# New node states turned by VectorE in 32x32 blocks, with x and the result moved in runs of 32 channels, and aggregation in four tiles

## The chip, the cores and the metric

The kernel runs on one core of one Trainium2 chip. The metric is device time in microseconds (us), the median of several runs: 2050.7 us for the kernel before (three runs, 2047.82 to 2055.25).

## The reference

Inputs are x (128 graphs, 128 nodes, 256 channels), adj (128 x 128 x 128, zeros and ones) and the weights of two layers, all in float32. Cut to what matters:

```python
# layer 0
h = relu(layernorm(x))
x_conv = relu(bn2(conv17(relu(bn1(conv1(h))))) + h)        # along the nodes
x_nmp  = exp(-dist(h @ w_se)) * adj @ relu(h @ w_msg + b_msg)
r, z   = sigmoid(...), sigmoid(...)                         # of [x_conv, x_nmp] @ w_ih + h @ w_hh
n      = tanh(gi_n + r * gh_n)
x      = x + (1 - z) * n + z * h                            # the new state
# layer 1, only on nodes 0 to 24
h = relu(layernorm(x))
for g, idx in enumerate(GROUPS):                            # 5 groups of nodes, 53 rows together
    A   = sym_normalized(adj[idx, idx] + I)
    hid = relu(A @ (h[idx] @ W1[g]) + b1[g])
    out = relu(A @ (hid @ W2[g]) + b2[g])
    x[idx] += softmax(fusion_w)[g] * out
```

Nodes 25 to 127 leave layer 1 as they came into it. So the kernel stores nodes 32 to 127 (96 of 128) right after layer 0, and only the first 32 nodes go on.

## The kernel before, in words

**Stages.** Stage A (layer norm, first convolution, Fourier transform along the nodes) and stage B (the 17-tap convolution as products per frequency) run twice, for two halves of the graphs. Beside them `early` makes the messages and aggregates of layer 0. Then stage C (`stage_c`, line 687) makes the gates and the new state, for 32 groups q of four graphs (GB = 4), 512 columns each, with channels on the partitions. Layer 1 (`prepare`, `block`, line 1009) runs in 8 blocks of 16 graphs beside stage C.

**What sets the order.** All engines run in program order, and the program order is written by a planner, `Order.run` (line 183). Each piece of work is a generator in a lane; it yields a pair: what the step costs TensorE in us, and how long to wait until its next step may be placed. The planner takes the lane that has had least (cost over weight) among those whose next step is due. In the last phase (line 1137) the lanes are `loads`, `groups` (stage C, two groups at a time), `beside`, `rows`, and `second` (layer 1, weight 0.2). A step that yields a small wait, as those of the wn products do (lines 833 to 853, 0.2 us), lets one step of another lane in. A DMA stands in its queue at the place where the planner put its step. SP's queue issues in order: a DMA that has to wait keeps back all behind it.

**End of a group in stage C.** r holds the sums for tanh. Line 855 (ScalarE) does tanh, lines 858 to 861 (POOL) make d = (h - n) * z and z = d + n, first for channels 128 to 255 (dc = 1), then for dc = 0. The last add reads columns in order (graph j, 32-node run t, node n) and writes (t, j, n). The tile d has the tag of u2 and u3, so the next group's u2 (line 766, ScalarE, a copy of the accumulator p1) takes the buffer of d with dc = 0. TensorE then goes on accumulating into p1 at line 788. Eight transposes on TensorE (line 878) turn z into rows of (graph, node), four tiles t by two halves dc, VectorE adds x to them from tile xt (lines 881 to 884), for t = 0 into the layer 1 state X1, and POOL's queue stores t = 1 to 3 (line 887). xt has one buffer and was loaded one group of steps earlier (line 809, `load_x`, four DMAs on SP, runs of 256 channels); its load waits until the stores of the group before have left the tile. A step after 11 us, before which the planner may place other work, separates the new state from the transposes (line 865).

**W1 in layer 1.** `block` takes the node groups in turn: `first(g)` is the hidden product (line 1038), `second(g)` the one with W2 (line 1047). `load_w1` (line 926, SP) loads W1 of group g + 2 into the buffer that `first(g)` has left, and its place in the program is right before `first(g + 1)` (line 1059). Two buffers hold W1.

**Aggregation in layer 1** is `gather` (line 1075): graphs lie in pairs a = 0, 1, and s = 0, 1 is the graph in its pair, at partitions 64 s. Both input and output of a product lie at partitions 64 s, so the four products use two 64 x 64 corners of the array, twice each. One PSUM tile takes all four. `fuse` (line 1086) folds the 53 rows to 32 nodes for each a.

Of the kernel before, what the change touches and what calls it, by code (L numbers as in the profile page):

```python
# [9 lines left out]
FP = mybir.dt.float32  # L10
AF = mybir.ActivationFunctionType
ALU = mybir.AluOpType
# [3 lines left out]
B, N, D = 128, 128, 256  # L16
# [3 lines left out]
P = 128  # L20
GB = 4
# [9 lines left out]
SB = 16  # L31
QS = SB // GB
# [6 lines left out]
NR = sum(SIZES)  # L39
NN = 25  # L40
RP = 64
WIDE = 32
# [50 lines left out]
def _constants():  # L93

    row_node = [n for g in GROUPS for n in g]
    row_group = [i for i, g in enumerate(GROUPS) for _ in g]
    fwd, inv, tap = _fourier()
    parts = {
        "ident": np.eye(P),
        "mhalf": np.full((P, 8), -0.5),  # L100
        "fwd": fwd, "tap": tap, "inv": inv,
        "ones2": np.kron(np.eye(2), np.ones((RP, RP))),
        "et": np.zeros((P, 2 * RP)),
        "same": np.zeros((P, RP)),
        "diag": np.zeros((P, RP)),
        "e4": np.zeros((P, P)),
        "s2": np.zeros((P, 2 * WIDE)),
        "grp": np.zeros((P, NG)),
        "sgrp": np.zeros((P, 2 * NG)),
        "grpt": np.zeros((P, P)),  # L110
        "sel": np.zeros((P, P)),
        "emb": np.zeros((P, 12)),
    }

    roles = {0: [(2, 2, 0), (0, 0, 1), (1, 1, 0), (0, 0, 1)],
             1: [(0, 0, -1), (0, 0, 1), (1, 1, 0), (1, 1, 0)],
             2: [(1, 1, 0), (1, 1, 0), (0, 0, -1), (0, 0, 1)]}
    for j in range(GB):
        for role, factors in roles.items():
            for ch in range(3):  # L120
                k = WIDE * j + 3 * role + ch
                parts["sel"][ch, k] = 1
                parts["emb"][k] = np.array(factors).T.reshape(-1)
    for r, (n, g) in enumerate(zip(row_node, row_group)):
        for s in range(2):
            k = s * RP + r
            parts["et"][n, k] = 1
            parts["same"][k, [i for i in range(NR) if row_group[i] == g]] = 1
            parts["diag"][k, r] = 1
            for j in (s, s + 2):  # L130
                parts["e4"][k, j * WIDE + n] = 1
            parts["s2"][k, s * WIDE + n] = 1
            parts["grp"][k, g] = 1
            parts["sgrp"][k, s * NG + g] = 1
            parts["grpt"][g, k] = 1
    at, o = {}, 0
    for name, a in parts.items():
        at[name] = (o, o + a.shape[1])
        o += a.shape[1]
    return np.concatenate(list(parts.values()), 1).astype(np.float32), at  # L140
# [67 lines left out]
def kernel(ctx: ExitStack, tc: tile.TileContext, x, adj, consts, vecs, w_se, conv1_w,  # L208
                    conv2_w, w_msg, b_msg, w_ih, w_hh, W1, W2, b2, fusion_w, out):
    nc = tc.nc  # L210
# [7 lines left out]
    ptmp = ctx.enter_context(tc.tile_pool(name="ptmp", bufs=5, space=PSUM))  # L218
# [14 lines left out]
    def c(name):  # L233
        a, b = CAT[name]
        return cst[:, a:b]

    def v(name, i=None):
        a, b = VAT[name]
        return vec[:, a:b] if i is None else vec[:, a + i:a + i + 1]

    ident = c("ident")
# [15 lines left out]
    s2w = cp.tile([P, 2 * WIDE], FP, name="s2w")  # L257
# [106 lines left out]
    lab, turn = ExitStack(), []  # L364
# [14 lines left out]
    def load_x(t, q):  # L379
        for j in range(GB):  # L380
            nc.sync.dma_start(out=t[j * WIDE:(j + 1) * WIDE],
                              in_=x[q * GB + j].rearrange("(t n) c -> n t c", n=WIDE))
# [186 lines left out]
    EN, IN, IN2, X1, E_DONE, F_DONE = {}, {}, {}, {}, set(), set()  # L569
# [117 lines left out]
    def stage_c(q):  # L687
# [9 lines left out]
        fr = LATE["co"]  # L697
        xi = fr.tile([P, 2, 512], FP, tag="tc", name=f"xi{q}")
        xc = fr.tile([P, 2, 512], FP, tag="xc", name=f"xc{q}")
        for h in range(2):  # L700
            yt = IN2.pop((q, h))
            pi = ptmp.tile([P, 2, 2, 4, WIDE], FP, tag="tmp", name=f"pi{q}_{h}")
            for n in range(4):
                o = n % 2 * WIDE
                for w in range(4):
# [4 lines left out]
                        start=True, stop=True)  # L710
# [3 lines left out]
            s = slice(h * D, (h + 1) * D)  # L714
# [41 lines left out]
        r = fr.tile([P, 2, 512], FP, tag="r", name=f"r{q}")  # L756
# [44 lines left out]
        z = fr.tile([P, 2, 512], FP, tag="z", name=f"z{q}")  # L801
# [3 lines left out]
        sigmoid(z2, z2, 2)  # L805
        some_sums(q + 1, 2)
        yield 2.6, 0.0
        xt = fr.tile([P, 4, D], FP, tag="xt", name=f"xt{q}")
        load_x(xt, q)
        nc.vector.tensor_tensor(z1, u3, product(wrz, 3, xs), ALU.add)  # L810
        sigmoid(z1, z1, 2)
        nc.vector.tensor_tensor(vt, vb, product(wh, 3, xh, ptmp), ALU.add)
# [41 lines left out]
        for dc in (1, 0):  # L854
            nc.scalar.activation(r[:, dc], r[:, dc], AF.Tanh, bias=v("b_ih", 4 + dc))  # L855

            d = fr.tile([P, 512], FP, tag=f"u{2 + dc}", name=f"d{q}_{dc}")
            nc.gpsimd.tensor_sub(d, hT[:, dc], r[:, dc])  # L858
            nc.gpsimd.tensor_mul(d, d, z[:, dc])
            pat = "p (j t n) -> p t j n"  # L860
            nc.gpsimd.tensor_add(z[:, dc].rearrange("p (t j n) -> p t j n", t=4, j=GB),
                                 d.rearrange(pat, j=GB, t=4),
                                 r[:, dc].rearrange(pat, j=GB, t=4))
        G_DONE.add(q)
        yield 0.87, 11.0


        blk = q // QS
        while blk > 2 and blk - 3 not in F_DONE:
            yield 0.0, 0.5  # L870
        if blk not in X1:
            X1[blk] = fr.tile([P, QS, D], FP, tag="x1", name=f"x1_{blk}", bufs=3)
        for h in range(2):
            po = ptmp.tile([P, 2, D], FP, tag="tmp", name=f"po{q}_{h}")
            for i in range(2):
                t = 2 * h + i
                for dc in (1, 0):
                    nc.tensor.transpose(po[:, i, dc * P:(dc + 1) * P],  # L878
                                        z[:, dc, t * P:(t + 1) * P], ident)
            if h == 0:  # L880
                nc.vector.tensor_add(X1[blk][:, q % QS], xt[:, 0], po[:, 0])
                nc.vector.tensor_add(xt[:, 1], xt[:, 1], po[:, 1])
            else:
                nc.vector.tensor_add(xt[:, 2:], xt[:, 2:], po)  # L884
        yield 0.9, 1.5
        for j in range(GB):
            nc.gpsimd.dma_start(out=out[q * GB + j, WIDE:].rearrange("(t n) c -> n t c", n=WIDE),  # L887
                                in_=xt[j * WIDE:(j + 1) * WIDE, 1:4])
        C_DONE.add(q)


# [55 lines left out]
    def prepare(blk):  # L947

        while not (blk - 1 in P_DONE and blk - 2 in {-2, *B1_DONE}):
            yield 0.0, 1.0  # L950
        pool, pool2, b1 = S["pool"], S["pool2"], S["b1"]
        ac, r4 = S["ac"][blk % 2], S["r4"][blk % 2]
        aj = pool.tile([NN, SB, NN], FP, tag="dd", name=f"aj{blk}")
        nc.sync.dma_start(out=aj, in_=adj[blk * SB:(blk + 1) * SB, :NN, :NN]
                          .rearrange("b n m -> n b m"))
        yield 0.0, 4.0

        for r, n, w in _runs():
# [10 lines left out]
        for p in range(SB // 2):  # L969
# [30 lines left out]
        pr4 = ptmp.tile([P, QS, 2, RP], FP, tag="tmp", name=f"pr4{blk}")  # L1000
        nc.tensor.matmul(pr4.rearrange("p q a r -> p (q a) r"), c("e4"), ac,
                         start=True, stop=True)
        for j in range(GB):
            s = slice(j * WIDE, (j + 1) * WIDE)
            nc.vector.tensor_copy(r4[s, :, j, :], pr4[s, :, j // 2, :NR])
        yield 0.9, 1.0
        P_DONE.add(blk)

    def block(blk):
        while not (blk in P_DONE and blk - 1 in B1_DONE):  # L1010
            yield 0.0, 0.5
        pool, yz, b2row = S["pool"], S["yz"], S["b2row"]
        w2, ac, r4 = S["w2"], S["ac"][blk % 2], S["r4"][blk % 2]
# [46 lines left out]
        x1 = X1[blk]  # L1060
# [13 lines left out]

        def gather(q):
            zt = zts[q]
            pg2 = ptmp.tile([P, 2, D], FP, tag="tmp", name=f"pg2{blk}_{q}")
            for a in range(2):
                for s in range(2):
                    rows = slice(s * RP, (s + 1) * RP)  # L1080
                    nc.tensor.matmul(pg2[rows, a], ac[rows, 2 * q + a], zt[rows, a],  # L1081
                                     start=True, stop=True)
            nc.vector.tensor_tensor(zt, pg2, b2row[:, None, :].to_broadcast([P, 2, D]), ALU.add)
            nc.scalar.activation(zt, zt, AF.Relu)

        def fuse(q):
            zt = zts.pop(q)
            pf = ptmp.tile([P, D], FP, tag="tmp", name=f"pfu{blk}_{q}")
            for a in range(2):
                nc.tensor.matmul(pf[a * 2 * WIDE:(a + 1) * 2 * WIDE], s2w, zt[:, a],  # L1090
                                 start=True, stop=True)
            nc.vector.tensor_add(x1[:, q], x1[:, q], pf)
            b0 = blk * SB + q * GB
            if blk < NBLK - 1:
                nc.gpsimd.dma_start(out=out[b0:b0 + GB, :WIDE], in_=x1[:, q])
                return
            for j in range(GB):
                eng = nc.scalar if q == QS - 1 and j % 2 else nc.sync
                eng.dma_start(out=out[b0 + j, :WIDE], in_=x1[j * WIDE:(j + 1) * WIDE, q])

        for what, q in ((turn, 0), (turn, 1), (turn, 2), (gather, 0), (turn, 3), (gather, 1),
                        (gather, 2), (fuse, 0), (gather, 3), (fuse, 1), (fuse, 2), (fuse, 3)):
            what(q)
            if (what, q) == (gather, QS - 1):
                B1_DONE.add(blk)
            yield {turn: 0.45, gather: 0.9, fuse: 0.5}[what], 0.5
        F_DONE.add(blk)


# [70 lines left out]
```

## Time and profile before

| what | value |
|---|---|
| median of 3 runs | 2050.7 us |
| profiled execution, its own time | 2049.36 us |
| its span | 2047.5 us |
| granted TensorE clock, mean | 0.995 |
| stage C and layer 1 beside it | 676 to 1960 us of the span |
| the last two blocks of layer 1 alone | from 1960 us |
| DMA packets | 190148, of them 23626 under 512 B |
| queue of SP (q1) / of POOL (q0) | 156942 / 32656 packets |

The page gives for each engine the busy time and its share of the span. A group line tells the source line, engine, operation, shapes, count, total and mean time of one, and the idle time before it with the engine that ended it. The chain follows the last instruction back to what released it. A timeline row is start, duration, engine, line, operation, and in brackets how long the engine was idle before and who released it; rows of the same kind are merged, with xN. A matmul in float32 shows as two instructions, a transpose as one.

### The profile page before, as it was taken

How to read it: one execution, taken by the hardware profiler on the slowest of the kernel's cores; microseconds unless marked ns; L12 is line 12 of the kernel's file. 1: busy time of each engine (PE TensorE's matmuls, PEld its weight loads, DVE VectorE, ACT ScalarE, POOL GpSimd, SP SyncE). 2: the span in 40 equal slices, each digit the busy share in tenths (PEclk: the TensorE clock that was granted, in tenths of full speed). 3: DMA queues.
4: the chain of work that ended last, by engine and by line, in shares of the span. 5: the costliest groups of instructions: out<-in, count | busy, mean ns of one | idle time of the engine just before them, and what ended most of it. 6: DMA issues, size and time to landing. Idle time of an engine off the chain costs nothing.

```text
span 2047.5 us, 34132 instructions
## 1 busy us (share of the span) xinstructions
PE 2006.3 (98%) x12852; PEld 1659.2 (81%) x12852; DVE 1285.1 (63%) x2775; ACT 688.5 (34%) x1547; POOL 741.3 (36%) x898
## 2 busy tenths in 40 slices
PE   7998999999999999999999999999999999999998
PEld 5667888888888888878788788878888888878875
DVE  6774445875433676757756776777567667766742
ACT  4663222454222344222222332232232323222333
POOL 3552665333655032422422233233224323233230
PEclk9999999999999999999999999999999999999999
DMA  9997788645777544431323232332332233323121
GB/s 217 295 284 229 265 267 281 191 162 185 253 256 245 152 127 131 116 108 53 87 73 91 75 84 83 101 80 76 83 88 78 76 98 90 86 78 104 39 71 52
DMA packets 190148, 281.91 MB, mean 138 GB/s; under 512 B 23626, under 2 KB 143375, under 8 KB 189983
## 3 DMA queue, kind: packets, MB, share of 16 engines
q1 hardware_dynamic: 156942, 185.46, 31.7%
q0 software_dynamic: 32656, 93.98, 14.5%
q8 instruction: 102, 1.67, 0.3%
q14 instruction: 64, 0.52, 0.1%
q10 hardware_dynamic: 384, 0.28, 0.1%
HBM read 187.34 MB, written 92.27 MB: 137 GB/s over the span
## 4 chain that ended last, share of the span: by engine, by line
PE 89%; DVE 3%; issue 3%; POOL 3%; DMA 2%; ACT 1%; SPq 0%; POOLq 0%; DVEq 0%; ACTq 0%
PE p L735 39%; PE pa L526 7%; PE pm L630 5%; PE ph L1038 5%; PE pz L1047 5%; PE pc L421 4%; PE pb L526 3%; PE pf L432 3%; PE px L656 3%; PE pi L706 3%; PE pg L1081 1%; PE pw L474 1%; PE po L878 1%; PE ph L410 1%; PE py L1021 1%
## 5 line engine op out<-in xcount | busy, mean ns | idle before, releaser
L858 POOL TENSOR_TENSOR d<-hTc,r 128x512 f32<-128x512 f32 x64 | 87.2, 1362 | 299.3 <-ACT r L855 288.7
L526 PE MATMUL pa<-wf,X 128*128 128x256 f32 x640 | 152.2, 381 | 0.0
L716 DVE SCALAR_TENSOR_TENSOR xc<-xi,s_bn,hTc 128x256 f32<-128x256 f32 x128 | 148.1, 1195 | 2.3
L558 DVE SCALAR_TENSOR_TENSOR y<-pa,kk 128x512 f32<-128x512 f32 x78 | 53.8, 690 | 151.4 <-ACT kk L557 151.4
L887 POOL DMA_DIRECT2D out<-xt x128 | 72.2, 569 | 172.5 <-DVE xt L884 169.3
L750 ACT ACTIVATE z<-z,brz 128x256 f32<-128x256 f32 x128 | 58.1, 501 | 221.3 <-DVE z L804 187.9
L735 PE MATMUL p<-tm,wrz 128*128 128x256 f32 x512 | 132.3, 381 | 0.0
L735 PE MATMUL p<-th,wrz 128*128 128x256 f32 x512 | 132.1, 380 | 0.0
L735 PE MATMUL p<-tc,wrz 128*128 128x256 f32 x512 | 131.8, 380 | 0.0
L526 PEld LDWEIGHTS pa<-wf,X 128*128 128x128 f32 x640 | 118.1, 190 | 16.2 <-issue 2.0
L630 PE MATMUL pm<-wmsg,hT 128*128 128x256 f32 x512 | 123.3, 386 | 0.0
L421 PE MATMUL pc<-c1w,hTa 128*128 128x256 f32 x512 | 121.4, 383 | 1.2 <-ACT hTa L412 1.2
L1040 ACT ACTIVATE hh<-ph,vec 128x96 f32<-128x96 f32 (+3 forms) x160 | 64.4, 403 | 147.0 <-PE ph L1038 137.8
L1038 PE MATMUL ph<-yz,w 128*128 128x96 f32 (+3 forms) x640 | 110.5, 327 | 1.9 <-issue 1.0
L719 ACT ACTIVATE xc<-xc,t_bn 128x256 f32<-128x256 f32 x128 | 64.8, 508 | 138.8 <-DVE xc L716 138.8
L630 PEld LDWEIGHTS pm<-wmsg,hT 128*128 128x128 f32 x512 | 97.3, 193 | 15.8 <-ACT kk L557 1.4
L421 PEld LDWEIGHTS pc<-c1w,hTa 128*128 128x128 f32 x512 | 94.3, 191 | 18.2 <-DVE h L424 4.8
L735 PEld LDWEIGHTS p<-tm,wrz 128*128 128x128 f32 x512 | 97.8, 191 | 13.5
L735 PE MATMUL p<-hTc,wrz 128*128 128x256 f32 x384 | 103.9, 393 | 5.0 <-ACT u L766 4.9
L735 PEld LDWEIGHTS p<-th,wrz 128*128 128x128 f32 x512 | 97.1, 190 | 13.6 <-PE p L735 0.2
L1038 PEld LDWEIGHTS ph<-yz,w 128*128 128x128 f32 x640 | 89.0, 195 | 23.3 <-issue 16.5
L1047 PE MATMUL pz<-hh,w 128*128 128x96 f32 (+3 forms) x640 | 107.3, 321 | 0.0
(200 smaller groups left out, 4566.1 us busy)
## 6 DMA issues: line engine op xcount, KB each, us to landing
wf<-wfd SPq DMA_DIRECT2D x160, 256.0 KB, 3.2
wfd<-ws POOLq DMA_DIRECT2D x64, 320.0 KB, 8.9
yd<-y POOLq DMA_DIRECT2D x80, 256.0 KB, 4.1
yt<-yd SPq DMA_DIRECT2D x64, 320.0 KB, 4.9
w<-in_W SPq DMA_DIRECT2D x40, 512.0 KB, 4.0
xa<-in_x SPq DMA_DIRECT2D x128, 128.0 KB, 5.2
hTd<-hTa POOLq DMA_DIRECT2D x32, 512.0 KB, 5.9
hT<-hTd SPq DMA_DIRECT2D x32, 512.0 KB, 6.3
```

What stands on the lines that cost most here:

```text
L421: nc.tensor.matmul(pc[:, i], hT[:, k, (2 * h + i) * N:(2 * h + i + 1) * N], c1w[:, k], start=(k == 0), stop=(k == 1))
L432: nc.tensor.matmul(pf[:, i, :F * NB], h1[:, 2 * h + i, k * P:(k + 1) * P], fwd, start=True, stop=True)
L526: nc.tensor.matmul(ps, xk(k), WF[f][:, k, s], start=(k == 0), stop=(k == 1))
L630: nc.tensor.matmul(pm[:, i], hT[:, k, j * N:(j + 1) * N], LATE["wmsg"][:, k], start=(k == 0), stop=(k == 1))
L716: nc.vector.scalar_tensor_tensor(xc[:, co, s], xi[:, co, s], scl["bn2"][:, co:co + 1], hT[:, co, s], op0=ALU.mult, op1=ALU.add)
L719: nc.scalar.activation(xc[:, co, s], xc[:, co, s], AF.Relu, bias=sft["bn2"][:, co:co + 1])
L735: nc.tensor.matmul(ps[:, m], w[:, i, k, m * P:(m + 1) * P], factor(i, x, t), start=first and j == 0, stop=last and j == len(n) - 1, skip_g ...
L858: nc.gpsimd.tensor_sub(d, hT[:, dc], r[:, dc])
L887: nc.gpsimd.dma_start(out=out[q * GB + j, WIDE:].rearrange("(t n) c -> n t c", n=WIDE), in_=xt[j * WIDE:(j + 1) * WIDE, 1:4])
L1038: nc.tensor.matmul(ph, w1[:, k, m * P:(m + 1) * P], yz[:, k, :, o:o + n], start=(k == 0), stop=(k == 1))
L1040: nc.scalar.activation(hh[:, m], ph, AF.Relu, bias=v("b1", g * 4 + m))
L1047: nc.tensor.matmul(pz, w2[:, g, m, cc * P:(cc + 1) * P], hs[g][:, m], start=(m == 0), stop=(m == 3))
```

## The change

Four things are done.

1. Only nodes 0 to 31 of the new state are turned on TensorE (two transposes per group instead of eight). The other 96 nodes are turned by VectorE, in 32 x 32 blocks: z is written so that a block holds 32 channels by 32 nodes that lie three apart (node 32 + 3 n + t), and the block turned has a node on a partition with 32 channels in a row. The last add on POOL becomes two, the second reading columns three apart.
2. x and the result for these nodes are moved in that layout: for each graph j and each block a of 32 channels one DMA with 32 partitions and 6 runs of 32 channels (128 bytes) each. The load has 20 DMAs on SP (four for nodes 0 to 31, straight into X1), the store 16, now on SP. VectorE's adds become one of 256 columns and one of 768.
3. In `gather`, graphs of a block are put in another order, so that the output of pair a lies at partitions 64 a and the four products use four corners of the array; each s has a PSUM tile of its own, and VectorE adds the bias in two instructions. The constants e4, the loads of adj (four DMAs for one) and the copies r4 follow that order.
4. The planner's costs follow: 0.22 instead of 0.9 for the transposes, 0.5 instead of 0.9 for a gather. The wait for a free X1 moves from the transposes' step to the load's.

```diff
@@ constants
-            for j in (s, s + 2):
+            for j in (2 * s, 2 * s + 1):
@@ stage_c, the load
-        xt = fr.tile([P, 4, D], FP, tag="xt", name=f"xt{q}")
-        load_x(xt, q)
+        while q // QS > 2 and q // QS - 3 not in F_DONE:
+            yield 0.0, 0.5
+        if q % QS == 0:
+            X1[q // QS] = fr.tile([P, QS, D], FP, tag="x1", name=f"x1_{q // QS}", bufs=3)
+        x1 = X1[q // QS][:, q % QS]
+        xt = fr.tile([P, GB, 6, WIDE], FP, tag="xt", name=f"xt{q}")
+
+        def slices(t, j):
+            return t[q * GB + j, WIDE:].rearrange("n c -> (n c)").rearrange(
+                "(n k a c) -> a n k c", k=6, a=4, c=WIDE)
+
+        for j in range(GB):
+            nc.sync.dma_start(out=x1[j * WIDE:(j + 1) * WIDE], in_=x[q * GB + j, :WIDE])
+            for a in range(4):
+                nc.sync.dma_start(out=xt[a * WIDE:(a + 1) * WIDE, j], in_=slices(x, j)[a])
@@ stage_c, the new state
-            pat = "p (j t n) -> p t j n"
-            nc.gpsimd.tensor_add(z[:, dc].rearrange("p (t j n) -> p t j n", t=4, j=GB),
-                                 d.rearrange(pat, j=GB, t=4),
-                                 r[:, dc].rearrange(pat, j=GB, t=4))
+            dn, rn = (a.rearrange("p (j n) -> p j n", j=GB) for a in (d, r[:, dc]))
+            nc.gpsimd.tensor_add(z[:, dc, :P].rearrange("p (j n) -> p j n", j=GB),
+                                 dn[:, :, :WIDE], rn[:, :, :WIDE])
+            pat = "p j (n t) -> p j t n"
+            nc.gpsimd.tensor_add(z[:, dc, P:].rearrange("p (j t n) -> p j t n", j=GB, t=3),
+                                 dn[:, :, WIDE:].rearrange(pat, t=3),
+                                 rn[:, :, WIDE:].rearrange(pat, t=3))
@@ stage_c, turning and storing
-        for h in range(2):
-            po = ptmp.tile([P, 2, D], FP, tag="tmp", name=f"po{q}_{h}")
-            for i in range(2):
-                t = 2 * h + i
-                for dc in (1, 0):
-                    nc.tensor.transpose(po[:, i, dc * P:(dc + 1) * P],
-                                        z[:, dc, t * P:(t + 1) * P], ident)
-            if h == 0:
-                nc.vector.tensor_add(X1[blk][:, q % QS], xt[:, 0], po[:, 0])
-                nc.vector.tensor_add(xt[:, 1], xt[:, 1], po[:, 1])
-            else:
-                nc.vector.tensor_add(xt[:, 2:], xt[:, 2:], po)
-        yield 0.9, 1.5
+        po = ptmp.tile([P, D], FP, tag="tmp", name=f"po{q}")
+        for dc in (1, 0):
+            nc.tensor.transpose(po[:, dc * P:(dc + 1) * P], z[:, dc, :P], ident)
+        zt = fr.tile([P, GB * 3, 2, WIDE], FP, tag="zt", name=f"zt{q}")
+        for dc in (1, 0):
+            nc.vector.transpose(zt[:, :, dc],
+                                z[:, dc, P:].rearrange("p (b n) -> p b n", n=WIDE))
+        nc.vector.tensor_add(x1, x1, po)
+        xtf = xt.rearrange("p j k c -> p (j k c)")
+        nc.vector.tensor_add(xtf, xtf, zt.rearrange("p b d c -> p (b d c)"))
+        yield 0.22, 1.5
         for j in range(GB):
-            nc.gpsimd.dma_start(out=out[q * GB + j, WIDE:].rearrange("(t n) c -> n t c", n=WIDE),
-                                in_=xt[j * WIDE:(j + 1) * WIDE, 1:4])
+            for a in range(4):
+                nc.sync.dma_start(out=slices(out, j)[a], in_=xt[a * WIDE:(a + 1) * WIDE, j])
@@ prepare
-        nc.sync.dma_start(out=aj, in_=adj[blk * SB:(blk + 1) * SB, :NN, :NN]
-                          .rearrange("b n m -> n b m"))
+        for i in range(GB):
+            nc.sync.dma_start(out=aj[:, i % 2 * 2 + i // 2::GB],
+                              in_=adj[blk * SB + i:(blk + 1) * SB:GB, :NN, :NN]
+                              .rearrange("b n m -> n b m"))
...
-            nc.vector.tensor_copy(r4[s, :, j, :], pr4[s, :, j // 2, :NR])
+            nc.vector.tensor_copy(r4[s, :, j % 2 * 2 + j // 2, :], pr4[s, :, j % 2, :NR])
@@ block
-            pg2 = ptmp.tile([P, 2, D], FP, tag="tmp", name=f"pg2{blk}_{q}")
+            pg2 = [ptmp.tile([P, D], FP, tag="tmp", name=f"pg2{blk}_{q}_{s}") for s in range(2)]
             for a in range(2):
                 for s in range(2):
                     rows = slice(s * RP, (s + 1) * RP)
-                    nc.tensor.matmul(pg2[rows, a], ac[rows, 2 * q + a], zt[rows, a],
-                                     start=True, stop=True)
-            nc.vector.tensor_tensor(zt, pg2, b2row[:, None, :].to_broadcast([P, 2, D]), ALU.add)
+                    nc.tensor.matmul(pg2[s][a * RP:(a + 1) * RP], ac[rows, 2 * q + a],
+                                     zt[rows, a], start=True, stop=True)
+            for s in range(2):
+                nc.vector.tensor_add(zt[:, s], pg2[s], b2row)
...
-            for a in range(2):
-                nc.tensor.matmul(pf[a * 2 * WIDE:(a + 1) * 2 * WIDE], s2w, zt[:, a],
+            for s in range(2):
+                nc.tensor.matmul(pf[s * 2 * WIDE:(s + 1) * 2 * WIDE], s2w, zt[:, s],
...
-            yield {turn: 0.45, gather: 0.9, fuse: 0.5}[what], 0.5
+            yield {turn: 0.45, gather: 0.5, fuse: 0.5}[what], 0.5
```

More of the change, by code (lines that the diff above doesn't have):

```diff
@@ L864, in stage_c @@
+            pat = "p j (n t) -> p j t n"
+            nc.gpsimd.tensor_add(z[:, dc, P:].rearrange("p (j t n) -> p j t n", j=GB, t=3),
+                                 dn[:, :, WIDE:].rearrange(pat, t=3),
+                                 rn[:, :, WIDE:].rearrange(pat, t=3))
         G_DONE.add(q)
         yield 0.87, 11.0
[L868 to L872, printed above, removed]
```

## The prediction

> **What bounds the kernel now.** I read the page's busy table first, then the chain that ended last, then the groups of instructions, then the timeline of single groups of stage C.
>
> ```profile
> PE 2006.3 (98%) x12852; PEld 1659.2 (81%) x12852; DVE 1285.1 (63%) x2775; ACT 688.5 (34%) x1547; POOL 741.3 (36%) x898
> ...
> PE 89%; DVE 3%; issue 3%; POOL 3%; DMA 2%; ACT 1%; SPq 0%; POOLq 0%; DVEq 0%; ACTq 0%
> ```
>
> TensorE sets the time: 98% busy, 89% of the chain. In stage C (from 676 to 1960 us by the stretch table, PE busy 1275.7 of 1284 us) a microsecond taken from TensorE is a microsecond off the span, unless another wait ends later. So two things are to be priced: what leaves TensorE, and which waits the change makes longer. POOL's 3% is the warning. Here is where it lies, in the timeline of one group boundary (start, us, engine, line, operation):
>
> ```profile
> 1381.50 1.34 POOL L859 TENSOR_TENSOR d<-d,z 128x512 f32<-128x512 f32 x1
> ...
> 1382.91 1.33 POOL L861 TENSOR_TENSOR z<-d,r 128x512 f32<-128x512 f32 x1
> ...
> 1384.28 0.60 ACT L766 ACTIVATE u<-p 128x512 f32<-128x512 f32 x1 [2.03 <-POOL z L861]
> ...
> 1384.93 1.13 PE L735 MATMUL p<-hTc,wrz 128*128 128x256 f32 x4 [0.35 <-ACT u L766]
> ```
>
> The buffer of u is the buffer of d of the group before. So L766 can't start before POOL's last add L861, and TensorE can't go on with p1 before L766: z's end, 0.04 us, ACT 0.60, TensorE. I went through all 31 boundaries in the timeline: in 17 TensorE starts 0.65 us after an L766 that itself started within 0.05 us of L861's end, in 2 more the same holds with TensorE still busy for some tenths, in one z is 0.3 us ahead, in 11 it is 1.3 us or more.
>
> The second place is SP's queue, in order (first the timeline of SP, then of TensorE, group 28):
>
> ```profile
> 1867.03 1.74 SPq L381 DMA_DIRECT2D xt<-in_x  x4
> 1868.82 12.46 SPq L926 DMA_DIRECT2D w<-in_W  x3
> ```
> ```profile
> 1860.58 1.04 PE L878 MATMUL po<-cst,z 128*128 128x128 f32 x8
> 1861.46 1.03 PE L735 MATMUL p<-tc,wrz 128*128 128x256 f32 x4
> ...
> 1878.93 1.94 PE L1038 MATMUL ph<-yz,w 128*128 128x96 f32 x16
> ```
>
> The first of the three w loads at 1868.82 holds W1 of the block's last node group; it lands about 4.0 us later (median of L926) and is used at 1878.93: 6.1 us to spare. The same order (xt load, w load, two hidden products in one stretch) stands in four blocks (at 1088, 1480, 1674 and 1868 us).
>
> **What the Trainium skill says.** (1) *TensorEngine Tiling (Array Packing)*, Tiling Modes and Gotcha 1: 64x64 gives four independent tiles; row tiles must not use one PSUM bank at the same time. The trace agrees as far as it goes: the eight instructions of L1081 use two tiles and take 1.01 us (1994.48 to 1995.49), where one after the other they would need 8 x 0.217 = 1.74 (price below); L643, four row tiles into four banks, starts eight 128-column instructions in 0.43 us (174.04 to 174.47), half of 8 x 0.109. (2) *GPSIMD Engine Reference*, Performance pitfalls: an SBUF read with a step over 8 bytes costs about half more per element (1.9 to 2.9 cycles). No instruction of this trace has such a step. (3) *DMA: Bandwidth & Descriptors*, Specifications: runs under 512 B miss line rate. Here only aj (100 B runs) shows such loads, see below. (4) *TensorE: Matmul & The Clock Gate*, Why this matters: no idle over some 3 us. The trace agrees: after a TensorE idle of 6.30 us ending at 167.51 the granted clock was 0.50 from 166 to 172 us, and 16 matmuls L630 took 5.5 us, not 3.5 to 3.7.
>
> **The change, part by part.**
>
> *Transposes on TensorE*, 8 to 2 per group. Above, 8 take 1861.46 - 1860.58 = 0.88 us, 0.109 each. 6 x 0.109 x 32 = **-20.9 us**. They lie in the saturated stretch, so all of it counts.
>
> *Aggregation*, 32 gathers. A 256-column instruction takes 0.217 (56 of L735 in 12.17 us in the chain). Now two tiles have four each: 0.87 of the 1.01. With four tiles, two each: 0.43. Saved 0.435 x 32 = **-13.9 us** (from 0, if tiles that share columns take turns, to -13.9; L643 speaks for the full value). VectorE's two adds of 128x256 for one of 128x512 (2 x 0.42 for 0.69) start that much earlier: 0.
>
> *VectorE.* Removed: L881, L882, L884, 0.42 + 0.41 + 0.68 = 1.51. Added: two transposes of 384 (L711 has 0.709 for 512; a 256-element add takes 0.42 and a 512-element one 0.69, so 128 elements are 0.135: about 0.57 each), an add of 256 (0.42), one of 768 (0.69 + 0.27 = 0.96): 2.5. Before L881 VectorE waited 1.7 to 2.4 us for po; z is ready then, so the transposes fit into that gap, and what follows po takes 1.38 instead of 1.51: 0. If the gap were gone, +1 us on 32 groups; VectorE is busy 26 of 40 us there, so I leave that out.
>
> *POOL.* Its four stores per group (0.56 us each) go; they weren't on the chain. But each of the two adds L861 becomes two: 128 elements, and 384 whose two inputs step by 3 elements = 12 bytes. POOL's times without such a step are 0.472 (128), 0.735 (256) and 1.817 (768), from L326: 2.11 ns per element, so 0.47 + 1.0 = 1.48 against 1.32: +0.16. With the half more of page (2) on the 384, an estimate, +0.40: +0.56 per add, +1.13 per group. If each of the two inputs paid that, it would be +1.6. The 17 boundaries above have no slack: 17 x 1.13 + 2 x 0.6 = **+20.4 us** (5.4 without the step's price, 31 at its upper end).
>
> *SP.* Loads go from 4 to 20 DMAs per group, and 16 stores come from POOL's queue to SP's. Four xt loads take 1.74 us, 0.435 each, and aj with 400 runs is followed by the next DMA after 0.44: the price is per DMA. 36 x 0.435 = 15.7 us a group. DMA time is no bound: around an xt load the windows' DMA share sums to 1.88 us (59 ns per 1 KB packet), with aj to 2.33, so 18 ns per 100 B packet; 12 packets per engine and DMA give 0.22, under 0.435. In group 28: VectorE ends at about 1862.1; 16 stores to 1869; landing 1.6 to 2.4, to 1871 (the loads wait for that, as the queue's waits show for xt, "SPq L381 <- DMA out<-xt", 519.2 us); 19 loads to 1879.2; then the w load, landed at 1883.2, wanted at 1878.93 - 0.66 = 1878.3. **TensorE waits 4.9 us**, with all that is in order behind it; by the clock row about 2.1 us more. Four blocks: 4 x 7 = **+28 us** (0, if the order of steps moves, to 60). Behind the same burst: aj of block 1, at 1003.57 now and read by POOL at 1010.08, would land near 1018, after the d of that group is due (1016.92): **+4** (0 to 6). hTc, xm and yt have 14 us and more to spare: 0. The xt load itself lands near 1881, wanted at 1900: 0.
>
> Sum: -20.9 - 13.9 + 20.4 + 28 + 4 = +17.6 on a profiled run of 2049.4 (span 2047.5 and 1.9 around it). The median shown, 2050.7, is 1.3 above that: **2068 us**.
>
> **Rivals.**
> A, faster: the w loads are not late. Place: the last W1 load of a block behind the burst. It decides if the burst of 35 DMAs shrinks by 4.9 us, 0.295 us per DMA, or if the planner puts that load ahead of it. For: the planner's costs change (0.9 to 0.22, 0.9 to 0.5). Against: the blocks repeat the order at a period of five groups, counted in steps and not in costs. -34.8 + 20.4 = -14.4: 2036.
> B, much slower: 128 B runs cost as much as 1 KB ones (59 ns). Then 12 x 59 = 0.71 us per DMA; the burst grows by 8.8 us, 4 x 8.8 = 35: 2103, and other loads follow. For: the stores are writes, which no row shows at this size. Against: aj's 18 ns.
> C, the step of 12 bytes is free on POOL: 15 less, 2053, no difference. A and C together: 2050.7 - 34.8 + 5.4 = 2021.
> D, the four tiles don't run together: up to 14 more, inside the forecast's own range.
>
> **Chances.** Forecast 0.48 (own range 2056 to 2085), A 0.13, B 0.22, C 0.12, A with C 0.05. About 0.3% (6 us) is what this measurement can tell from no change. Faster: A and A with C, less what of A comes near: 0.16. Same: C's most and some of A: 0.14. Slower: 0.70. The range 2034 to 2106 leaves out A with C, a part of A, and about 0.09 of B.
>
> **What would show it.** po x64 instructions instead of 256; L1081's eight in 0.57 us. The strided add on POOL at 1.4 us (forecast) or 1.0 (C), and the idle of u's write put down to POOL z in 17 or more boundaries. SP with 16 and 20 DMAs in a row at 0.43 us each (0.7: B), and waits of ph for w of some 5 us four times, with a lower clock after them; none of these: A. I am wrong if TensorE's idle in stage C is still about 8 us, or if VectorE shows as its releaser.

## The result, and the profile after

The changed kernel takes 2138.2 us (median of 4 runs, 2128.6 to 2143.8) against 2050.5: a ratio of 1.0422, 95% interval 1.0400 to 1.0444, so it is slower by 86.5 us. The profiled execution took 2141.8 us, span 2140.0. Below, differences between kernels are given as the difference of their ratios times 2050.5 us, because the kernel before was measured again beside each set of runs.

The page of the changed kernel: busy time, granted clock by slice, share of the chain that ended last.

```profile
PE 2000.6 (93%) x12660; PEld 1649.2 (77%) x12660; DVE 1336.2 (62%) x2839; ACT 686.6 (32%) x1547; POOL 707.7 (33%) x834
...
PEclk9998999999999999999899999999999989998999
...
PE 34%; POOL 10%; SPq 7%; issue 5%; DVE 2%; DMA 2%; ACT 1%; DVEq 0%; POOLq 0%; ACTq 0%
```

TensorE was 98% busy and is 93% now: 139.4 us of the span are idle (2140.0 - 2000.6), against 41.2 before. GpSimd has gone from 3% to 10% of the chain, and SP's queue, which had 0%, has 7%. TensorE's busy time is only 5.7 us lower although 192 instructions left it: work takes longer where the granted clock is low (digit 8 in the clock row). The waits of the changed kernel (who waited for whom: us in all, times, longest) name the places:

```profile
ACT u L766 <- POOL z L877: 64.6, 24, 5.7
...
PEld p L735 <- ACT u L766: 47.2, 23, 4.8
...
POOL b L970 <- DMA aj<-in_adj: 45.4, 4, 19.2
...
PE p L735 <- ACT u L766: 38.2, 23, 4.4
...
PE ph L1049 <- DMA w<-in_W: 36.5, 5, 12.2
```

In the kernel before, the first and the fourth of these were much smaller, and the third and fifth were not among its waits:

```profile
ACT u L766 <- POOL z L861: 17.5, 17, 2.0
...
PE p L735 <- ACT u L766: 4.9, 7, 1.8
```

So all three predicted mechanisms are there: GpSimd's chain, W1 behind SP's row, and the adjacency behind it. The last is 45.4 us as a wait of GpSimd's, where the prediction put 4 us on the time.

The five W1 waits last 3.4, 5.6, 12.2, 11.9 and 3.4 us. Here is the longest, in the timeline of VectorE, of SP (start, us, queue, line, operation, count; some loads left out) and of TensorE:

```profile
1730.10 0.96 DVE L893 TENSOR_TENSOR xt<-xt,zt 128x768 f32<-128x768 f32 x1
```
```profile
1731.09 10.32 SPq L897 DMA_DIRECT2D out<-xt  x16
1741.58 0.46 SPq L820 DMA_DIRECT2D x<-in_x  x1
1742.93 3.07 SPq L822 DMA_DIRECT2D xt<-in_x  x4
...
1755.58 7.92 SPq L935 DMA_DIRECT2D w<-in_W  x3
```
```profile
1741.70 1.92 PE L1049 MATMUL ph<-yz,w 128*128 128x96 f32 x16
...
1759.39 3.70 PE L1049 MATMUL ph<-yz,w 128*128 128x96 f32 x16 [12.23 <-DMA w<-in_W]
```

VectorE has the result at 1731.06; SP needs 24.5 us, until 1755.58, to get to W1, and TensorE stands still for 12.23 us. Its next 16 hidden products take 3.70 us where the 16 before took 1.92. The stretches show why (columns: stretch; length; busy us and count of five engines; granted clock; DMA share; GB/s):

```profile
1731.10:1741.40 10.30, 10.30 (x49) 8.93 (x48) 7.91 (x19) 2.40 (x6) 0.55 (x1) 1.00 0.23 33
...
1759.40:1763.20 3.80, 3.80 (x17) 3.80 (x18) 0.00 (x0) 1.09 (x4) 0.00 (x0) 0.50 0.19 73
```

After this idle time of 12.23 us the granted clock is 0.50, in agreement with the Trainium skill (*TensorE: Matmul & The Clock Gate*, Why this matters: no idle gaps of TensorE over some 3 us). And while SP issues its 16 stores the DMA engines are 23% busy, so they are not what makes SP slow.

GpSimd's adds, and the two parts that were to gain, in the groups of the changed kernel (busy us, mean ns of one):

```profile
L877 POOL TENSOR_TENSOR z<-d,r 128x384 f32<-128x384 f32 x64 | 96.9, 1513 | 0.0
...
L874 POOL TENSOR_TENSOR z<-d,r 128x128 f32<-128x128 f32 x64 | 32.4, 506 | 5.0
...
L1092 PE MATMUL pg<-zt,ac 64*64 64x256 f32 x256 | 21.2, 401 | 0.0
...
L886 PE MATMUL po<-cst,z 128*128 128x128 f32 x64 | 12.4, 276 | 0.0
```

The same parts of the kernel before:

```profile
L861 POOL TENSOR_TENSOR z<-d,r 128x512 f32<-128x512 f32 x64 | 84.4, 1319 | 5.0
...
L1081 PE MATMUL pg<-zt,ac 64*64 64x256 f32 x256 | 34.2, 388 | 0.0
...
L878 PE MATMUL po<-cst,z 128*128 128x128 f32 x256 | 33.2, 273 | 0.0
```

GpSimd's one add of 1.319 us became two of 0.506 and 1.513. Aggregation fell by 13.0 us and the transposes by 20.8: the gain on TensorE, 33.8 us, is there as busy time in the groups; all of it, and 86 us more, is lost elsewhere.

### The profile page after: what moved, and what is told of

The parts are those of the page before. It is cut to its first block, busy times and chain, and to the rows that moved or that the text cites. A ratio compares the mean times of both kernels' runs of the same rounds, so it can differ in the third digit from the quotient of the medians.

```text
span 2140.0 us, 34789 instructions
## 1 busy us (share of the span) xinstructions
PE 2000.6 (93%) x12660; PEld 1649.2 (77%) x12660; DVE 1336.2 (62%) x2839; ACT 686.6 (32%) x1547; POOL 707.7 (33%) x834
## 4 chain that ended last, share of the span: by engine, by line
PE 34%; POOL 10%; SPq 7%; issue 5%; DVE 2%; DMA 2%; ACT 1%; DVEq 0%; POOLq 0%; ACTq 0%
PE p L735 22%; PE ph L1049 4%; PE pz L1058 4%; SPq L897 3%; POOL z L877 3%; SPq L822 3%; POOL d L872 3%; POOL d L871 3%; POOL z L874 1%; DMA w<-in_W 1%; PE py L1032 1%; PE pi L706 1%; DMA out<-xt 1%; DMA aj<-in_adj 1%; PE pg L1092 1%
## 5 line engine op out<-in xcount | busy, mean ns | idle before, releaser
L1049 PE MATMUL ph<-yz,w 128*128 128x96 f32 (+3 forms) x640 | 119.4, 345 | 39.2 <-DMA w<-in_W 36.5
L735 PE MATMUL p<-th,wrz 128*128 128x256 f32 x512 | 133.0, 383 | 11.5 <-DVE r L863 10.4
L1049 PEld LDWEIGHTS ph<-yz,w 128*128 128x128 f32 x640 | 96.0, 211 | 61.8 <-issue 52.0
L735 PE MATMUL p<-hTc,wrz 128*128 128x256 f32 x384 | 106.3, 400 | 38.2 <-ACT u L766 38.2
L716 DVE SCALAR_TENSOR_TENSOR xc<-xi,s_bn,hTc 128x256 f32<-128x256 f32 x128 | 138.7, 1122 | 2.3
L948 POOL TENSOR_TENSOR rs<-rs,cst 128x1 f32<-128x1 f32 x32 | 18.3, 571 | 330.2 <-DVE rs L947 318.7
L735 PEld LDWEIGHTS p<-hTc,wrz 128*128 128x128 f32 x384 | 69.0, 192 | 61.5 <-ACT u L766 47.2
L735 PEld LDWEIGHTS p<-tc,wrz 128*128 128x128 f32 x512 | 96.2, 193 | 17.9 <-DVE tc L586 5.8
## 6 DMA issues: line engine op xcount, KB each, us to landing
wfd<-ws POOLq DMA_DIRECT2D x64, 320.0 KB, 11.5
```

Of the source, the lines that this page charges most:

```text
L716: nc.vector.scalar_tensor_tensor(xc[:, co, s], xi[:, co, s], scl["bn2"][:, co:co + 1], hT[:, co, s], op0=ALU.mult, op1=ALU.add)
L735: nc.tensor.matmul(ps[:, m], w[:, i, k, m * P:(m + 1) * P], factor(i, x, t), start=first and j == 0, stop=last and j == len(n) - 1, skip_g ...
L1049: nc.tensor.matmul(ph, w1[:, k, m * P:(m + 1) * P], yz[:, k, :, o:o + n], start=(k == 0), stop=(k == 1))
```

## The experiments

All are edits of the changed kernel, except the four-tile one (e4). Ratios are to the kernel before, measured beside each. e1, e3, e6, e9 and e12 leave out the reference's order of nodes or channels in the result and serve only to measure; the others keep it.

| run | median us | ratio (95% interval) | against the changed kernel, us | TensorE idle, us | clock |
|---|---|---|---|---|---|
| changed kernel | 2138.2 | 1.0422 (1.0400 to 1.0444) | | 139.4 | 0.974 |
| e1, runs of 768 B | 2084.9 | 1.0153 (1.0112 to 1.0194) | -55 | 92.2 | 0.985 |
| e6, 9 DMAs for 36 | 2055.3 | 1.0011 (0.9991 to 1.0030) | -84 | 79.1 | 0.993 |
| e2, W1 and adjacency on ScalarE | 2070.7 | 1.0088 (1.0057 to 1.0119) | -68 | 81.8 | 0.988 |
| e10, W1 alone | 2088.2 | 1.0178 (1.0156 to 1.0201) | -50 | 96.7 | 0.984 |
| e11, adjacency alone | 2124.1 | 1.0348 (1.0318 to 1.0378) | -15 | 122.7 | 0.973 |
| e3, add in runs of 32 | 2112.8 | 1.0296 (1.0263 to 1.0329) | -26 | 117.9 | 0.977 |
| e12, one add | 2103.6 | 1.0251 (1.0227 to 1.0274) | -35 | 102.3 | 0.976 |
| e9, e6 and e3 | 2036.0 | 0.9927 (0.9901 to 0.9952) | -101 | 55.8 | 0.994 |
| e4, kernel before + four tiles | 2042.6 | 0.9957 (0.9944 to 0.9970) | | 49.4 | 0.992 |
| e8, e2 and step on VectorE | 2048.8 | 0.9984 (0.9973 to 0.9995) | -90 | 66.7 | 0.990 |
| e8x, e8 and one load of 32 nodes | 2055.0 | 1.0016 (1.0004 to 1.0028) | -83 | 66.4 | 0.989 |
| e7, stores on GpSimd | 2136.2 | 1.0421 (1.0384 to 1.0458) | 0 | 131.5 | 0.977 |
| e13, e7 and two xt | 2067.1 | 1.0068 (1.0045 to 1.0092) | -73 | 86.3 | 0.988 |
| e17, two xt alone | 2123.0 | 1.0348 (1.0320 to 1.0376) | -15 | 120.1 | 0.978 |
| e14, e13 and step on VectorE | 2042.6 | 0.9949 (0.9930 to 0.9969) | -97 | 63.0 | 0.992 |
| e16, e14 and e2 | 2044.9 | 0.9971 (0.9955 to 0.9986) | -92 | 64.7 | 0.993 |

### What SP takes per DMA, and what that costs

e1 leaves 36 DMAs and all bytes, and changes only the runs:

```diff
-                "(n k a c) -> a n k c", k=6, a=4, c=WIDE)
+                "(a n k c) -> a n k c", k=6, a=4, c=WIDE)
```

> The changed kernel, with the 96 nodes' x and result moved in one run of 768 bytes per partition in place of six of 128; still 36 DMAs and the same bytes per group (the channels land in other places, so the result's rows are not the reference's). Theory, the number of runs sets what SP takes per DMA: SP takes 0.435 us per DMA as in the loads before, not 0.645, a group's 36 end 7.6 us sooner, TensorE's waits for W1 fall from 36.5 to under 12 us in all, and the time falls from 2138 to about 2100. Rival, SP takes 0.64 us per DMA whatever its runs: the 16 stores still take 10.3 us, the waits for W1 stay above 30 us, and the time stays within 8 us of 2138.

The time fell by 55 us, somewhat more than the theory's 38. SP's timeline in e1:

```profile
1742.49 7.30 SPq L897 DMA_DIRECT2D out<-xt  x16
1749.83 0.42 SPq L820 DMA_DIRECT2D x<-in_x  x1
1750.97 1.72 SPq L822 DMA_DIRECT2D xt<-in_x  x4
```

16 stores take 7.30 us, 0.456 each, with a median of 0.419, near the forecast's 0.435; in the changed kernel it was 0.645 each, with a median of 0.602. TensorE's wait for W1 is 11.6 us in 2 places for 36.5 in 5. So DMAs of this shape keep SP itself longer with runs of 128 bytes, and that is worth 55 us.

e6 keeps the 128-byte runs and makes the DMAs fewer:

```diff
-                "(n k a c) -> a n k c", k=6, a=4, c=WIDE)
+                "(b p c) -> p b c", b=6, c=WIDE)
...
-            for a in range(4):
-                nc.sync.dma_start(out=slices(out, j)[a], in_=xt[a * WIDE:(a + 1) * WIDE, j])
+            nc.sync.dma_start(out=slices(out, j), in_=xt[:, j])
```

> The changed kernel with 9 DMAs per group in place of 36: one load of the 32 nodes, and one load and one store per sample of 128 partitions x 6 runs of 128 bytes; the same bytes and the same 128-byte packets (the channels land in other places, so the result's rows are not the reference's). Theory, SP's loss is the number of DMAs: 9 x 0.65 = 6 us per group instead of 23, TensorE's wait for W1 falls from 36.5 to under 5, GpSimd's for the adjacency from 45 to under 15, and the time falls from 2138 to about 2080. Rival, the 128-byte packets themselves are the cost, on SP or on the DMA engines: the four stores together still take SP or the engines about 10 us, the waits for W1 stay above 20 us and the time above 2120.

SP's timeline at one boundary of e6:

```profile
1722.04 2.45 SPq L895 DMA_DIRECT2D out<-xt  x4
1724.54 0.56 SPq L819 DMA_DIRECT2D x<-in_x  x1
1726.64 2.16 SPq L821 DMA_DIRECT2D xt<-in_x  x4
```

Four stores of 768 runs take 2.45 us, where 16 of 192 took 10.32. The price isn't per run: it is 0.55 us (median) for 768 runs over 128 partitions, 0.60 for 192 over 32, and 0.42 for 32 long runs. Nor do short runs alone make a DMA dear: an adjacency load of the changed kernel, 100 runs of 100 bytes over 25 partitions, takes 0.34. The wait for W1 is gone, the one for the adjacency is 2.0 us, and with them go 84 us, 26 more than the theory had: the whole share of SP's row. The number of DMAs and their shape both count, through the time until W1's turn comes.

### Which loads behind the row cost it

```diff
-            nc.sync.dma_start(out=S["w1", n], in_=W1[n % NG].rearrange("(k p) o -> p k o", p=P))
+            nc.scalar.dma_start(out=S["w1", n], in_=W1[n % NG].rearrange("(k p) o -> p k o", p=P))
...
-            nc.sync.dma_start(out=aj[:, i % 2 * 2 + i // 2::GB],
+            nc.scalar.dma_start(out=aj[:, i % 2 * 2 + i // 2::GB],
```

Both (e2), the first alone (e10), the second alone (e11):

> The changed kernel with only the W1 and adjacency loads issued by ScalarE instead of SP; all 36 DMAs of a group stay on SP. Theory, their place behind the 36 on SP costs the time: TensorE's wait for W1 falls from 36.5 to under 5 us and GpSimd's wait for the adjacency from 45.4 to under 10, the halved clock after the waits goes too, and the time falls from 2138 to about 2080 (36 of waits, some 20 of clock and adjacency). Rival, the DMA engines are full of small packets and a load from any queue is late: both waits keep more than two thirds of their size and the time stays above 2120. If the rest of the loss is GpSimd's chain, 30 us above the kernel before (2080) remains.

> The changed kernel with only the W1 loads issued by ScalarE; the adjacency stays behind the 36 DMAs on SP. Forecast's theory (W1 is most of SP's loss, the adjacency small): of the 67 us that both moves won together, W1 alone wins 55 or more, about 2080. Rival, the adjacency is a wait of its own of the size of its 45 us on GpSimd: W1 alone wins 35 to 45, about 2098, and GpSimd's wait for the adjacency stays near 45.

> The changed kernel with only the adjacency loads issued by ScalarE; W1 stays on SP. Forecast's theory: they are worth no more than 12 us, 2126 or more, and TensorE's wait for W1 stays near 36. Rival: 25 us or more, 2113 or less; then the two loads are two losses that add up to the 67.

Both win 68 us, W1 alone 50, the adjacency alone 15; the two add up to 65, so they are two losses side by side. W1's is the larger; both results lie between the two expectations for them. In e10 the wait for W1 is gone and the adjacency's stays:

```profile
ACT u L766 <- POOL z L877: 65.7, 25, 5.7
...
POOL b L970 <- DMA aj<-in_adj: 48.7, 4, 19.9
```

In e2 the 36 DMAs stand on SP as before, at the same 0.60 us. So their place ahead of W1 and the adjacency is the cause, and not full DMA engines, which would have made a load of any queue late: with W1 on ScalarE no wait of TensorE for it is left. Of e6's 84 us, 16 more than e2's 68 are not tied to a load. The two profiles differ by 12.1 us, 9.4 of them in TensorE's busy time (1986.3 for 1976.9, with a mean clock of 0.988 for 0.993). In e2 GpSimd still waits 14.9 us for the adjacency, and ScalarE waits 75.4 us for z where it is 65.9 in e6. ScalarE's issuing of the loads in its own program order may be the reason, but no run tests that, and it stays open.

e7 takes the 16 stores off SP:

```diff
-                nc.sync.dma_start(out=slices(out, j)[a], in_=xt[a * WIDE:(a + 1) * WIDE, j])
+                nc.gpsimd.dma_start(out=slices(out, j)[a], in_=xt[a * WIDE:(a + 1) * WIDE, j])
```

> The changed kernel with the 16 stores of a group issued by GpSimd, as the 4 stores of the kernel before are; the loads stay on SP. Theory, it is the 36 in one row on SP that make W1 and adjacency late: 16 x 0.6 = 10 us fewer ahead of them, the wait for W1 (12 us at most) falls under 8 us in all, and the time falls to about 2085, because GpSimd is idle then. Rival, GpSimd's own chain is what TensorE waits for, and 16 issues of 0.7 us ahead of the next group's work, 8.6 us more than the 4 of before, come into it: slower than 2138.

Neither expectation came true: the time didn't move, and W1 was about as late as before (32.0 us in 4 places). SP's own waits show why, first in e7, and then in e13, which is e7 with `bufs=2` for xt:

```profile
SPq L822 <- DMA out<-xt: 658.1, 84, 30.5
```
```profile
SPq L683 <- PE p L735: 420.1, 30, 25.7
SPq L935 <- PE ph L1049: 272.5, 29, 21.4
```

> The changed kernel with the stores issued by GpSimd and two buffers for xt, so that no x load waits for the stores of the group just before. Theory, in the earlier run with the stores on GpSimd the W1 loads were late because the x loads ahead of them waited for the stores: with two buffers SP's wait for the stores falls from 658 us to under 100, TensorE's wait for W1 from 32 to under 5, and the time falls to about 2085, as W1 and adjacency moved to ScalarE gave 2071 with the stores on SP. Rival, 16 issues on GpSimd cost its chain as much as they take off SP: the wait for W1 goes, and the time stays above 2120.

With one xt, SP stood in e7 at the x loads until the stores of the group before had landed, and W1 stood behind the 20 loads. With two buffers, that wait is 8.0 us, none for W1 is left among TensorE's, and the time is 73 us below e7's. Is the one buffer then the cause by itself? e17 changes only that:

> The changed kernel with two buffers for xt and nothing else: stores, loads, W1 and adjacency all stay on SP in the same order. Theory, order: SP takes its DMAs in turn and stands at the stores until VectorE has the result, so the loads and W1 behind them are as late as before; TensorE's wait for W1 stays above 25 us and the time above 2125. Rival, the one buffer is the cause in itself: the time falls to about 2067, as with the stores on GpSimd.

It wins 15 us, a little more than expected, and W1 is still 31.8 us late: the stores, which must wait for VectorE, stand in SP's row ahead of W1, with a second buffer or without. SP's own waits in e17:

```profile
SPq L897 <- DVE u L792: 330.6, 28, 18.9
```

In these runs W1 was in time when both the stores and the single buffer were gone (e13), when W1 left the row (e2, e10), or when the row was short (e6).

### GpSimd's adds

e3 takes the step of 12 bytes away, e12 the second instruction too:

```diff
-            pat = "p j (n t) -> p j t n"
+            pat = "p j (t n) -> p j t n"
```

> The changed kernel with GpSimd's last add of the 96 nodes reading d and r in runs of 32 (nodes 32t to 32t+31 as block t) instead of every third node; nothing else is changed, so the results of the 96 nodes go to other nodes' rows. Theory, the step of 12 bytes costs GpSimd 0.5 us of the 1.51 us add, and this add stands at the end of the chain that TensorE waits for: the add takes about 1.0 us, ScalarE's wait for it falls from 64.6 us to about 30, and the time falls from 2138 by 24 x 2 x 0.5 = 24 us to about 2114. Rival, the two adds cost by their number and not by the step: the add stays above 1.4 us and the time within 5 us of 2138. Rival, the add is shorter and nobody waits for it: 1.0 us, time within 5 us of 2138.

> The changed kernel with GpSimd's two adds per half made one again, as in the kernel before (512 elements, runs of 32, 1.32 us), so the 96 nodes' results go to other rows and samples. Theory: against the add in runs of 32 in two instructions (2113; 0.51 + 1.12 us) the single one is 0.31 us shorter, 0.62 per chain, over some 20 chains 12 us: 2101, and the whole of GpSimd's share in the loss is then 37 us. Rival, only the step mattered: within 4 us of 2113.

The group of e3:

```profile
L877 POOL TENSOR_TENSOR z<-d,r 128x384 f32<-128x384 f32 x64 | 72.0, 1125 | 0.0
```

The add takes 1125 ns for 1513: the step costs 0.39 us an instruction and 26 us in all, and the split into two (0.506 + 1.125 for 1.319) some 9 us more, where the intervals of e3 and e12 just overlap. ScalarE's wait for z fell from 64.6 to 47.1 in e3 (30 was expected) and to 23.6 in e12. TensorE's wait for u fell from 38.2 to 10.0 in e12. GpSimd's whole share is 35 us.

### The parts together

> The changed kernel with 9 DMAs per group and GpSimd's add in runs of 32, both earlier edits together (channels and nodes land in other places). Theory, the two losses stand side by side: 2055 - 25 = 2030, which is below the kernel before, and what the fewer transposes and the four tiles save comes to light. Rival, the two overlap (without SP's wait GpSimd's chain is hidden, or the other way round): above 2045.

e9 runs the same 12660 TensorE instructions as the changed kernel:

```profile
PE 1975.5 (97%) x12660; PEld 1632.1 (80%) x12660; DVE 1314.3 (65%) x2839; ACT 687.0 (34%) x1547; POOL 683.9 (34%) x834
```

Span 2031.3. Of the 108.7 us between the two spans 83.6 are TensorE's idle time (139.4 - 55.8), and 25.1 are the same instructions at a lower clock (2000.6 - 1975.5; mean clock 0.974 for 0.994). Against the kernel before, TensorE's busy time is 30.8 us lower, near the 34.8 of the forecast, and the idle 14.6 higher. The time was 6 us above the 2030 expected: e6 and e3 alone won 84 and 26, both together 101, so about 9 us of the two overlap.

e4 puts the four-tile hunks alone into the kernel before:

```diff
-                    nc.tensor.matmul(pg2[rows, a], ac[rows, 2 * q + a], zt[rows, a],
-                                     start=True, stop=True)
+                    nc.tensor.matmul(pg2[s][a * RP:(a + 1) * RP], ac[rows, 2 * q + a],
+                                     zt[rows, a], start=True, stop=True)
```

> The kernel before with only the aggregation in four 64 x 64 tiles (adjacency order, e4, two banks per gather, two adds of the bias); x, result and the transposes of the 96 nodes as before. Forecast's theory: the 256 aggregation matmuls take 13.9 us less of TensorE and nothing is lost, so 2050.5 - 14 = 2037. Rival, the tiles don't run side by side in this order: their busy time stays near 34 us and the time within 4 us of 2050. Rival, the four adjacency loads or the second add cost what is won: within 4 us of 2050 with a shorter aggregation.

The aggregation's group in e4:

```profile
L1083 PE MATMUL pg<-zt,ac 64*64 64x256 f32 x256 | 21.2, 401 | 0.0
```

The four tiles run side by side (21.2 us busy for 34.2), and 8.8 us of the 13.0 come out (6.2 to 11.5 by the interval), between the theory's 14 and the rivals' 4. Where the rest goes, no run says.

### The layout of the reference, without the losses

e8 is e2 with the step in VectorE's reads; e8x joins four loads.

```diff
-            pat = "p j (n t) -> p j t n"
-            nc.gpsimd.tensor_add(z[:, dc, P:].rearrange("p (j t n) -> p j t n", j=GB, t=3),
-                                 dn[:, :, WIDE:].rearrange(pat, t=3),
-                                 rn[:, :, WIDE:].rearrange(pat, t=3))
+            nc.gpsimd.tensor_add(z[:, dc, P:].rearrange("p (j n) -> p j n", j=GB),
+                                 dn[:, :, WIDE:], rn[:, :, WIDE:])
...
-            nc.vector.transpose(zt[:, :, dc],
-                                z[:, dc, P:].rearrange("p (b n) -> p b n", n=WIDE))
+            nc.vector.transpose(zt[:, :, dc].rearrange("p (j t) n -> p j t n", t=3),
+                                z[:, dc, P:].rearrange("p (j n t) -> p j t n", j=GB, t=3))
```

> The changed kernel with W1 and adjacency loads issued by ScalarE, and the step over every third node moved from GpSimd's add to the reads of VectorE's two transposes; the result is laid out as in the reference. Theory, the step on VectorE lies beside other work: GpSimd's add takes 1.0 to 1.1 us, and 2071 - 25 = 2046 follows, even if each transpose takes some 0.4 us longer. Rival, the step makes the transposes so slow (over 1.5 us each) that the stores and VectorE's next sums come late: above 2060.

> The same with the four loads of the 32 nodes joined into one: 33 DMAs per group for 36. Theory, once no load that TensorE waits for stands behind them, SP's burst is hidden: within 5 us of the kernel of the same call that keeps four loads. Rival, what remains on SP (other loads of the next group) still waits: 1.8 us per group less, 10 us or more faster.

> The same, with the step over every third node moved to the reads of VectorE's transposes. Theory, the losses add: 25 us less than with the step on GpSimd, about 2060. Rival, GpSimd is now held by the stores and not by the add: less than 10 us gained.

> The same again, with W1 and adjacency loads issued by ScalarE besides. Theory, nothing that TensorE waits for is behind SP then: 2036, as in the run with 9 DMAs and runs of 32, and below the kernel before. Rival, the issues on GpSimd and ScalarE cost what SP gives up: no faster than 2049, the time with stores on SP, W1 and adjacency on ScalarE and the step on VectorE.

VectorE's transposes in the changed kernel and in e8:

```profile
L889 DVE STREAM_TRANSPOSE zt<-z 128x384 f32<-128x384 f32 x64 | 33.1, 555 | 4.7 <-POOL z L877 4.7
```
```profile
L887 DVE STREAM_TRANSPOSE zt<-z 128x384 f32<-128x384 f32 x64 | 41.0, 677 | 3.8 <-POOL z L876 3.8
```

A transpose takes 677 ns for 555, and GpSimd's add 1123 for 1513: the step costs VectorE 0.12 us where it cost GpSimd 0.39, and VectorE has time to spare (65% busy). e8 is about level with the kernel before (3 us faster by the ratio). e8x was 6.6 us slower than e8 by the ratios, not within 5. In the profiles TensorE's idle time is the same (66.4 us for 66.7), and its busy time is 5.5 us higher (1986.3 for 1980.8); what causes this, no run says. e14 won 24 us by the step, as the theory said, and ended 17 below what was expected (2060), because e13 was already 18 below its own: at 0.9949 it is faster than both kernels by its interval, level with e4. e16 won nothing over e14 (the intervals overlap) and ended 9 us above the 2036 expected: with two buffers and the stores off SP nothing that TensorE waits for was left behind SP, as e14's waits, with none for W1 or the adjacency, also say.

## Why the prediction was wrong

The sign and the places of the losses were right; the time lies above the range because the price of a DMA on SP, and with it what W1 and the adjacency lose, was taken too small, and GpSimd's share too.

**TensorE's gain** (-20.9 and -13.9): right as busy time, -20.8 and -13.0 in the groups. As time, e4 gave 8.8 us of the second (6.2 to 11.5), less than forecast; "all of it counts" was not tried for the transposes alone.

**SP** (+28, with +4 for the adjacency): 84. The step that failed is "the price is per DMA", 0.435 us, taken from the xt loads and from aj. It was read off DMAs of another shape. The 0.44 for aj was misread besides: where another DMA followed at once, it started 0.36 to 0.39 us after aj in the kernel before. Stores and x loads in runs of 128 bytes took 0.60 (medians; the 16 stores of the row shown average 0.645), and even the 32-node loads between them, 1 KB runs whose kind takes 0.42 in e1, took 0.59 (median).

At the longest wait the forecast's own line of reasoning with the measured times comes out right: from VectorE's end to W1 it had 17.1 us; measured are 24.5, 7.4 more; 4.9 + 7.4 = 12.3 against the 12.23 in the timeline. A second wait (11.9) is like it; the other three (3.4, 5.6 and 3.4) are not, so this reasoning covers two of the five places. e1, which has the price of the forecast, runs at 2085, inside the range. With the longer row W1 is late in five places and not four, and the adjacency in four and not one. By the runs W1 is worth 50 us (e10) for the forecast's 28, and the adjacency 15 (e11) for 4. And the clock was too cheap: between the changed kernel and e6 the same instructions differ by 23.7 us of busy time (2000.6 - 1976.9) beside 60.3 of idle time, where the forecast had four times 2.1.

**Rival B** had a price near the measured one (0.71) and said "other loads follow". Its mechanism was wrong: the DMA engines were 23% busy while SP issued the stores, and e2 has W1 in time with all the small packets still there.

**GpSimd** (+20.4): 35. The price of the 12-byte step was right: 0.39 us measured, 0.40 estimated from the Trainium skill (*GPSIMD Engine Reference*, Performance pitfalls: half more per element for such a read; here the whole add took 1513 ns for 1125, a third more). Two other terms were too small: 384 elements without a step take 1.125 us and not 1.00, so an add got 0.70 longer (0.506 + 1.513 - 1.319) and not 0.56; and ScalarE waited for z at 24 boundaries, not 17 and 2: 24 x 1.40 = 34. A chain that grows by 1.4 us reaches boundaries that had some slack before. Rival C fell with e3.

**VectorE** (0): right in itself, though it shows as a releaser, which the forecast named as a sign of being wrong:

```profile
PE p L735 <- DVE r L863: 10.4, 1, 10.4
...
PE p L735 <- DVE tc L586: 5.6, 1, 5.6
```

Both waits are in e10 (11.1 and 7.8), which keeps the adjacency on SP. In e2, e6 and e11, which have it earlier, neither is above 1.0 us. So they come from the late adjacency, and their sum of 16.0 us is near the 15 that e11 won. **Rival D** fell with e4, **A** (W1 not late) with the profile itself.

The account: +84 (e6) and +35 (e12), less 33.8 on TensorE, would be +85, and +86.5 was measured. That agreement is in part luck, for the terms add up only roughly: e9 shows an overlap of some 9 us, e4 gave 8.8 of 13.0 us as time, and 16 of the 84 are not tied to a load. The two profiles also differ by 5.5 us in TensorE's wait for the load of the tile hT early in the kernel (11.8 for 6.3); its code is unchanged, and it was 6.6 us in e10 and 12.1 in e6, so it isn't the change's.

## What to carry to other kernels

A queue that issues in order is a resource like an engine: before moving many small DMAs to it, add up the time until the load behind them that the busiest engine needs, with the issue time of just that shape, and see what they themselves wait for (a result, a landed store, a single buffer). If no trace has the shape, carry the price as a range through the wait, because the wait is a difference of two long times: at the place shown, 48% on the price made 150% on the wait. A pattern with a step belongs on the engine that has slack, not on the one that ends a chain: moved from GpSimd to VectorE, it gave 21 us (e8 against e2) and 24 (e14 against e13).

## What the runs showed of the hardware

- SP took 0.42 us for a DMA of 32 runs of 768 bytes, 0.60 for 192 runs of 128 bytes over 32 partitions, and 0.55 for 768 runs of 128 bytes over 128 partitions. Loads of 100 runs (changed kernel) and of 400 runs (kernel before) of 100 bytes over 25 partitions both took 0.34 (all medians). What in the shape sets the time was not tried further.
- A load of 32 runs of 1 KB took SP 0.59 us (median) among DMAs of short runs and 0.42 among DMAs of long ones; the seven in the changed kernel that came after a pause of SP or behind another kind of DMA took 0.34 to 0.46. So a DMA's issue time depends on its neighbours.
- The same 12-byte step over 384 elements cost GpSimd's add of two inputs 0.39 us and VectorE's 32x32 transpose 0.12.
